# Layer 2's score products on the two halves of the array's rows, and C's product on quarters of the array

## Chip, cores, metric

One Trainium2 chip, one core of it in use. The metric is the device time of one execution in microseconds (us); lower is better.

## The reference

64 graphs of 256 nodes and width 512 pass four layers in f32. Every layer is `x = x + layer(relu(layernorm(x)))`. The change touches layer 2, which has 8 heads of width 64:

```python
Xp = einsum('bnd,hdk->bhnk', X, Wp) + bp
Xc = einsum('bhnk,hjk->bhnj', Xp, C)                                   # "C's product"
attn = tanh(A[:, None] * einsum('bhnj,bhmj->bhnm', Xc, Xp))            # "score products"
Xh = einsum('bhnm,bhmk->bhnk', attn, Xp)
out = relu(moveaxis(Xh, 1, 2).reshape(...))
```

Layer 0 and layer 3 gate a product by a softmax over nodes. Layer 1 is graph attention: its sums e_self[i] + e_neigh[j] are made by a small product with 40 rows.

## The kernel before

The weights stay on the chip, and each graph goes through all four layers there. Two graphs are interleaved; the build orders the instructions of both, so the order on an engine is not the written one. Two heads of 64 share the 128 partitions. To serve both with one product, the kernel pads with zeros: C is a 128x128 block with two 64x64 blocks on its diagonal, and Xc stands in a buffer whose other half of columns is zero for each head.

```python
    # The C of two heads on the diagonal of a block.
    c2_s = consts.tile([P, HP, P], F32)
    nc.gpsimd.memset(c2_s, 0.0)
    ...
    # Layer 2's Xc of two heads, apart by columns so that one product serves both.
    xc = consts.tile([P, HP, 2, N], F32)
    nc.gpsimd.memset(xc, 0.0)
    ...
        # layer 2, one graph; xpt is Xp transposed: [128 = two heads, pair of heads, node]
        for q in range(HP // 2):
            pc = passing("pc").rearrange("p (s n) -> p s n", s=2)
            for s in range(2):
                nc.tensor.matmul(pc[:, s, :], c2_s[:, 2 * q + s, :], xpt[:, 2 * q + s, :], start=True, stop=True)
            nc.vector.tensor_copy(xc[0:U, 2 * q:2 * q + 2, 0, :], pc[0:U])
            nc.scalar.copy(xc[U:P, 2 * q:2 * q + 2, 1, :], pc[U:P])
        ...
        for p in range(HP):
            th = []
            for m in range(NC):
                ps = passing("ps")
                nc.tensor.matmul(ps, xpt[:, p, m * P:(m + 1) * P], xc[:, p], start=True, stop=True)
                t = pairs.tile([P, 2, N], F32, name="th", bufs=6)
                nc.vector.tensor_tensor(t, ps.rearrange("p (s n) -> p s n", s=2),
                                        at[:, m, None, :].to_broadcast([P, 2, N]), OP.mult)
                nc.scalar.activation(t, t, AF.Tanh)
                th.append(t)
            if waiting is not None:
                spread(*waiting)      # the products with Xp for the pair of heads before
            waiting = (p, th)
```

Layer 1's product, whose two operands have 40 partitions (KE):

```python
                nc.tensor.matmul(ps, left[:, i * P:(i + 1) * P], right[:, 2 * p:2 * p + 2, :],
                                 start=True, stop=True)
```

## Time and profile before

| | before |
|---|---|
| time, median | 7153.95 us (7152.99 to 7154.43, 4 runs) |
| TensorE busy | 6468.8 us, 90% of the span |
| VectorE, ScalarE, GpSimd busy | 41%, 28%, 9% |
| mean granted clock of TensorE | 0.892 |
| score products, C's product | 510 us, 128 us busy |

How to read it. In the page's groups and in the timeline, a row names the line of the kernel, the engine, the operation, what it writes and reads, the shapes (partitions x elements), how many, and then busy time and mean ns of one (groups), or start and length in us (timeline, at the start of the row). L355 is the score product, L336 C's product, L287 layer 1's 40-row product. In the changed kernel they are L355, L334 and L282. A matmul's listed length is longer than what it costs in a stream (0.592 us listed for 512 columns, 0.429 to the next start), so costs are read from start to start. The lines themselves are in the prediction.

### The profile page before, as it was taken

The numbers are of one execution on the slowest core, as the hardware profiler recorded it, in microseconds if no ns is written. First come the engines' busy times: TensorE is split into PE (matmuls) and PEld (weight loads), VectorE is DVE, ScalarE is ACT, GpSimd is POOL, SyncE is SP. The second block draws the span as 40 slices with busy tenths as digits, with TensorE's granted clock in tenths as the row PEclk, the third lists the DMA queues.
The fourth block names the chain that finished last, engine by engine and source line by source line (L and its number), as shares of the span: only waits on it lengthen the run. The fifth ranks groups of instructions, "written<-read, shape, count | busy, mean of one in ns | idle before, by whom it ended". The sixth has DMA issues, their size and how long they took to land. (4 is left out here: it accounts for less than half of the span.)

```text
span 7152.9 us, 64137 instructions
## 1 busy us (share of the span) xinstructions
PE 6468.8 (90%) x24578; PEld 3687.2 (52%) x24578; DVE 2966.5 (41%) x7510; ACT 1997.0 (28%) x4801; POOL 671.6 (9%) x590
## 2 busy tenths in 40 slices
PE   7989999899998999989989999899989998999988
PEld 4555555555555555555555555555555554555554
DVE  4444444444444444434444344443444434444443
ACT  2222222222322222222222222232222222222222
POOL 1101001010010000100010001000010010100100
PEclk8988988889888898888988889888888888898889
DMA  2000000000000000000000000000000000000000
GB/s 66 15 11 12 12 11 15 12 11 12 11 15 12 11 15 8 15 12 11 15 11 12 15 8 15 11 12 15 8 15 12 11 15 11 12 12 11 11 6 6
DMA packets 55970, 95.80 MB, mean 13 GB/s; under 512 B 12080, under 2 KB 29040, under 8 KB 55664
## 3 DMA queue, kind: packets, MB, share of 16 engines
q1 hardware_dynamic: 34816, 50.34, 2.2%
q0 software_dynamic: 9216, 33.56, 1.2%
q10 hardware_dynamic: 11632, 7.80, 0.4%
q8 instruction: 195, 3.19, 0.2%
q14 instruction: 111, 0.91, 0.0%
HBM read 58.13 MB, written 33.55 MB: 13 GB/s over the span
## 5 line engine op out<-in xcount | busy, mean ns | idle before, releaser
L175 PE MATMUL pf<-wqk_s,ht 128*128 128x512 f32 x2048 | 1043.7, 659 | 0.0
L175 PE MATMUL pf<-w_s,ht 128*128 128x512 f32 x2048 | 981.4, 635 | 1.0
L175 PE MATMUL pv<-wv_s,ht 128*128 128x512 f32 x2048 | 945.2, 597 | 0.0
L167 PE MATMUL pt<-ident,hn 128*128 128x128 f32 x2048 | 414.3, 361 | 458.6 <-DVE hn L161 453.3
L281 PEld LDWEIGHTS po<-feats,et 128*128 128x128 f32 x4096 | 584.9, 218 | 314.4 <-ACT et L275 148.1
L299 ACT ACTIVATE e<-e,nmx 128x256 f32<-128x256 f32 x1024 | 510.3, 499 | 666.0 <-DVE nmx L296 665.9
L281 PE MATMUL po<-feats,et 128*128 128x64 f32 x4096 | 632.4, 305 | 43.9 <-ACT et L275 43.9
L175 PEld LDWEIGHTS pf<-wqk_s,ht 128*128 128x128 f32 x2048 | 418.2, 215 | 487.4 <-issue 487.2
L175 PEld LDWEIGHTS pf<-w_s,ht 128*128 128x128 f32 x2048 | 403.5, 203 | 514.4 <-issue 497.9
L287 PE MATMUL ps<-right,left 40*128 40x512 f32 x1024 | 660.1, 734 | 0.0
L167 PEld LDWEIGHTS pt<-ident,hn 128*128 128x128 f32 x2048 | 332.8, 192 | 544.4 <-issue 499.7
L168 ACT ACTIVATE ht<-pt 128x512 f32<-128x512 f32 x512 | 294.2, 596 | 1131.2 <-PE pt L167 1131.2
L291 ACT ACTIVATE e<-ps 128x512 f32<-128x512 f32 x512 | 305.7, 597 | 1073.6 <-PE ps L287 1069.4
L292 DVE TENSOR_TENSOR e<-ps,e 128x512 f32<-128x512 f32 x512 | 348.4, 685 | 549.4 <-ACT e L291 549.4
L348 PEld LDWEIGHTS ph<-xp,th 128*128 128x128 f32 x4096 | 492.5, 192 | 100.8 <-issue 69.1
L175 PEld LDWEIGHTS pv<-wv_s,ht 128*128 128x128 f32 x2048 | 364.6, 190 | 337.7 <-issue 337.7
L359 ACT ACTIVATE th<-th 128x512 f32<-128x512 f32 x512 | 321.2, 627 | 713.3 <-DVE th L357 713.3
L355 PE MATMUL ps<-xc,xpt 128*128 128x512 f32 x1024 | 510.1, 617 | 0.5 <-ACT xc L338 0.5
L277 DVE COPY et<-pt 128x512 f32<-128x512 f32 x256 | 177.0, 691 | 781.2 <-PE pt L271 781.2
L271 PE MATMUL pt<-ident,e 128*128 128x128 f32 x2048 | 387.8, 313 | 119.0 <-ACT e L299 117.3
L348 PE MATMUL ph<-xp,th 128*128 128x64 f32 x4096 | 495.3, 273 | 0.0
L271 PEld LDWEIGHTS pt<-ident,e 128*128 128x128 f32 x2048 | 255.0, 158 | 456.4 <-issue 186.8
(89 smaller groups left out, 5929.3 us busy)
## 6 DMA issues: line engine op xcount, KB each, us to landing
x_in<-in_x_dram SPq DMA_DIRECT2D x64, 512.0 KB, 3.4
out_dram<-xt POOLq DMA_DIRECT2D x64, 512.0 KB, 3.2
adj_in<-in_adj_dram SPq DMA_DIRECT2D x64, 256.0 KB, 2.7
wqk_s<-in_L_gnn_Wqk_dram ACTq DMA_DIRECT2D x1, 2048.0 KB, 10.6
wv_s<-in_L_gnn_W_v_dram ACTq DMA_DIRECT2D x1, 1024.0 KB, 9.7
w_s<-in_L_gnn_W_dram ACTq DMA_DIRECT2D x4, 256.0 KB, 8.5
w_s<-in_L_gnn_Wp_dram ACTq DMA_DIRECT2D x4, 256.0 KB, 6.5
wv_s<-in_L_gnn_Wv_dram ACTq DMA_DIRECT2D x1, 1024.0 KB, 12.5
```

The lines of the kernel that those rows point to most:

```text
L167: nc.tensor.transpose(pt[:, k * P:(k + 1) * P], hn[:, c, k * P:(k + 1) * P], ident)
L168: nc.scalar.activation(ht[:, :, c * P:(c + 1) * P], pt.rearrange("p (k i) -> p k i", k=KC), AF.Relu)
L175: nc.tensor.matmul(p, ht[:, k, c * P:(c + 1) * P], w[:, k], start=(k == 0), stop=(k == KC - 1))
L271: nc.tensor.transpose(pt[:, q * P:(q + 1) * P], e[:, s, j * P:(j + 1) * P], ident)
L281: nc.tensor.matmul(po[:, h * U:(h + 1) * U], et[:, s, j, :], feats[:, j, h * U:(h + 1) * U], start=(j == 0), stop=(j == NC - 1))
L287: nc.tensor.matmul(ps, left[:, i * P:(i + 1) * P], right[:, 2 * p:2 * p + 2, :], start=True, stop=True)
L291: nc.scalar.activation(e, psv, AF.Copy, scale=0.2)
L292: nc.vector.tensor_tensor(e, psv, e, OP.max)
L299: nc.scalar.activation(e[:, s, :], e[:, s, :], AF.Exp, bias=nmx[:, s:s + 1], scale=-1.0, accum_out=sums[:, 2 * p + s:2 * p + s + 1])
L348: nc.tensor.matmul(ph[n][:, h * U:(h + 1) * U], th[m][:, s, n * P:(n + 1) * P], xp[:, m, h * U:(h + 1) * U], start=(m == 0), stop=(m == NC ...
L355: nc.tensor.matmul(ps, xpt[:, p, m * P:(m + 1) * P], xc[:, p], start=True, stop=True)
L359: nc.scalar.activation(t, t, AF.Tanh)
```

## The change

Its intent: stop streaming zeros. Each head of a pair uses its own 64 rows of the array; the products of the two heads should run at once. For C's product each head uses a 64x64 quarter. Each half writes its own PSUM bank.

```diff
-    # The C of two heads on the diagonal of a block.
-    c2_s = consts.tile([P, HP, P], F32)
-    nc.gpsimd.memset(c2_s, 0.0)
+    c2_s = consts.tile([P, HP, U], F32)
     for s in range(2):
-        nc.scalar.dma_start(c2_s[s * U:(s + 1) * U, :, s * U:(s + 1) * U], ...)
+        nc.scalar.dma_start(c2_s[s * U:(s + 1) * U], ...)
@@ (xc and its zeros leave the constants; xc is now a working tile [P, HP, N])
         for q in range(HP // 2):
-            pc = passing("pc").rearrange("p (s n) -> p s n", s=2)
-            for s in range(2):
-                nc.tensor.matmul(pc[:, s, :], c2_s[:, 2 * q + s, :], xpt[:, 2 * q + s, :], start=True, stop=True)
-            nc.vector.tensor_copy(xc[0:U, 2 * q:2 * q + 2, 0, :], pc[0:U])
-            nc.scalar.copy(xc[U:P, 2 * q:2 * q + 2, 1, :], pc[U:P])
+            pc = [passing("pc").rearrange("p (a n) -> p a n", a=2) for _ in range(2)]
+            for a in range(2):
+                for s in range(2):
+                    half = slice(s * U, (s + 1) * U)
+                    nc.tensor.matmul(pc[s][half, a, :], c2_s[half, 2 * q + a, :],
+                                     xpt[half, 2 * q + a, :], start=True, stop=True)
+            nc.vector.tensor_copy(xc[0:U, 2 * q:2 * q + 2, :], pc[0][0:U])
+            nc.scalar.copy(xc[U:P, 2 * q:2 * q + 2, :], pc[1][U:P])
@@
         for p in range(HP):
+            ps = [passing("ps").rearrange("p (m n) -> p m n", m=NC) for _ in range(2)]
+            for m in range(NC):
+                for s in range(2):
+                    half = slice(s * U, (s + 1) * U)
+                    nc.tensor.matmul(ps[s][:, m, :], xpt[half, p, m * P:(m + 1) * P], xc[half, p, :],
+                                     start=True, stop=True)
             th = []
-            for m in range(NC):
-                ps = passing("ps")
-                nc.tensor.matmul(ps, xpt[:, p, m * P:(m + 1) * P], xc[:, p], start=True, stop=True)
-                t = pairs.tile([P, 2, N], F32, name="th", bufs=6)
-                nc.vector.tensor_tensor(t, ps.rearrange("p (s n) -> p s n", s=2), at[:, m, None, :]..., OP.mult)
+            for s in range(2):
+                t = pairs.tile([P, NC, N], F32, name="th", bufs=6)
+                nc.vector.tensor_tensor(t, ps[s], at, OP.mult)
                 nc.scalar.activation(t, t, AF.Tanh)
```

More of the change, by code (lines that the diff above doesn't have):

```diff
@@ L90, in tile_four_gnn_layers @@
     nc.scalar.dma_start(b2_bc, b2.rearrange("h u -> (h u)").partition_broadcast(P))
-    c2_s = consts.tile([P, HP, P], F32)
-    nc.gpsimd.memset(c2_s, 0.0)
+    c2_s = consts.tile([P, HP, U], F32)
     for s in range(2):
-        nc.scalar.dma_start(c2_s[s * U:(s + 1) * U, :, s * U:(s + 1) * U],
-                            c2t.rearrange("(a s) k j -> s k a j", s=2)[s])
+        nc.scalar.dma_start(c2_s[s * U:(s + 1) * U], c2t.rearrange("(a s) k j -> s k a j", s=2)[s])
     wqk3_s = load_weight("wqk3_s", wqk3)
@@ L135, in tile_four_gnn_layers @@
     nc.vector.tensor_copy(right[0:H], own[0:H, :, None].to_broadcast([H, H, N]))
-    xc = consts.tile([P, HP, 2, N], F32)
-    nc.gpsimd.memset(xc, 0.0)
     held = set()
@@ L331, in graph @@
             nc.scalar.copy(xpt[:, :, c * P:(c + 1) * P], pt.rearrange("p (k i) -> p k i", k=HP))
-        hold("layer 2")
+        xc = work.tile([P, HP, N], F32, name="xc")
         for q in range(HP // 2):
-            pc = passing("pc").rearrange("p (s n) -> p s n", s=2)
-            for s in range(2):
-                nc.tensor.matmul(pc[:, s, :], c2_s[:, 2 * q + s, :], xpt[:, 2 * q + s, :], start=True, stop=True)
-            nc.vector.tensor_copy(xc[0:U, 2 * q:2 * q + 2, 0, :], pc[0:U])
-            nc.scalar.copy(xc[U:P, 2 * q:2 * q + 2, 1, :], pc[U:P])
+            pc = [passing("pc").rearrange("p (a n) -> p a n", a=2) for _ in range(2)]
[6 more added lines that the diff above has]
+            nc.scalar.copy(xc[U:P, 2 * q:2 * q + 2, :], pc[1][U:P])
         yield
@@ L347, in spread @@
                     for m in range(NC):
-                        nc.tensor.matmul(ph[n][:, h * U:(h + 1) * U], th[m][:, s, n * P:(n + 1) * P],
+                        nc.tensor.matmul(ph[n][:, h * U:(h + 1) * U], th[s][:, m, n * P:(n + 1) * P],
                                          xp[:, m, h * U:(h + 1) * U], start=(m == 0), stop=(m == NC - 1))
         for p in range(HP):
-            th = []
-            for m in range(NC):
-                ps = passing("ps")
-                nc.tensor.matmul(ps, xpt[:, p, m * P:(m + 1) * P], xc[:, p], start=True, stop=True)
-                t = pairs.tile([P, 2, N], F32, name="th", bufs=6)
-                nc.vector.tensor_tensor(t, ps.rearrange("p (s n) -> p s n", s=2),
-                                        at[:, m, None, :].to_broadcast([P, 2, N]), OP.mult)
+            ps = [passing("ps").rearrange("p (m n) -> p m n", m=NC) for _ in range(2)]
[4 more added lines that the diff above has]
+                                     start=True, stop=True)
+            th = []
+            for s in range(2):
+                t = pairs.tile([P, NC, N], F32, name="th", bufs=6)
+                nc.vector.tensor_tensor(t, ps[s], at, OP.mult)
                 nc.scalar.activation(t, t, AF.Tanh)
@@ L365, in graph @@
         spread(*waiting)
-        held.remove("layer 2")
         xn = work.tile([P, NC, D], F32, name="xt", bufs=4)
```

## The prediction

> **What bounds the kernel now.** I read the page's busy table first, then the slices with the granted clock, the groups of instructions by line, the timeline of TensorE in the middle of the run, and the waits.
>
> ```profile
> span 7152.9 us, 64137 instructions
> ...
> PE 6468.8 (90%) x24578; PEld 3687.2 (52%) x24578; DVE 2966.5 (41%) x7510; ACT 1997.0 (28%) x4801; POOL 671.6 (9%) x590
> ...
> PEclk8988988889888898888988889888888888898889
> ...
> L287 PE MATMUL ps<-right,left 40*128 40x512 f32 x1024 | 660.1, 734 | 0.0
> ...
> L355 PE MATMUL ps<-xc,xpt 128*128 128x512 f32 x1024 | 510.1, 617 | 0.5 <-ACT xc L338 0.5
> ...
> L336 PE MATMUL pc<-xpt,c_s 128*128 128x256 f32 x512 | 127.6, 392 | 29.7 <-ACT xpt L331 28.7
> ```
>
> TensorE is busy 90% of the span and nothing else passes half of it apart from its own weight loads. The remaining 10%, 684 us, is idle time in front of a few lines. So time taken off TensorE is time off the span, except in places where TensorE would only wait longer for something else. The chain on the page covers only the last few per cent and carries nothing here. The two groups that the change touches are 510 us (score products) and 128 us (C's product), 9% of the span together. That is the ceiling of what can be discussed.
>
> Each f32 product appears as two weight loads and two matmuls: 64 graphs x 4 pairs of heads x 2 chunks are 512 score products, and the group counts 1024. The timeline gives the real rate, because the listed duration of one matmul includes a pipeline tail:
>
> ```profile
> 3548.43 1.95 PE L175 MATMUL pq<-wqk_s,ht 128*128 128x128 f32 x16
> 3550.21 1.88 PE L355 MATMUL ps<-xc,xpt 128*128 128x512 f32 x4
> 3551.93 2.74 PE L175 MATMUL pv<-wv_s,ht 128*128 128x512 f32 x6
> ```
>
> From the start of the four score matmuls to the start of the next group are 1.72 us, so 0.43 us for each 512-column matmul. (Subtracting the listed 0.592 of the last from 1.88 and dividing by three gives the same 0.429.) The 256-column matmuls of C's product follow each other at 0.216 us. Streaming of columns is what these cost; a weight load (0.19 us listed, one every 0.11 us where the 64-column products of layer 2 queue for it) hides behind it.
>
> The kernel already has a product on part of the rows, the 40-row sum of layer 1:
>
> ```profile
> 3508.70 1.12 PE L287 MATMUL ps<-right,left 40*128 40x512 f32 x2
> 3509.76 0.66 PE L271 MATMUL pt<-ident,e 128*128 128x128 f32 x4
> ...
> 3680.16 1.88 PE L355 MATMUL ps<-xc,xpt 128*128 128x512 f32 x4
> 3681.97 1.12 PE L287 MATMUL ps<-right,left 40*128 40x512 f32 x2
> 3683.02 1.98 PE L355 MATMUL ps<-xc,xpt 128*128 128x512 f32 x4
> 3684.84 1.89 PE L348 MATMUL ph<-xp,th 128*128 128x64 f32 x16
> ```
>
> Here the reader sees what a visit to another shape of the array costs. From 3680.16 to 3681.97 are 1.81 us where four matmuls stream in 1.72: 0.09 us are lost on entering the 40-row product. Its two matmuls last 1.05 us to the next start instead of 0.86; of the 0.19 too much, 0.10 is a weight load that could not run ahead (the second starts 1.12 - 0.59 = 0.53 after the first), and 0.09 is lost on leaving. The next full-array product again shows its first weight load: 1.98 instead of 1.88. So one visit loses 0.09 + 0.10 + 0.09 + 0.06 to 0.10, about 0.37 us.
>
> **What the Trainium skill says.** "TensorEngine Tiling (Array Packing)", section Key Properties: "Changing tiling mode (not just tile) drains the TensorE". The trace agrees, at the 0.37 us just read. "TensorE: Matmul & The Clock Gate", section "Part 3: Packing small matmuls — row/col tiling": matmuls on different row groups run concurrently, weight loads for another row group are pulled ahead, but matmuls start and end strictly in program order. No run so far shows two row groups at once; my main risk is here. "FP8 and Floating Point Precision", section "TensorE Precision Notes": true FP32 takes four passes. The trace agrees in effect: two instructions per product, each at 429 ns for 512 columns, twice the 213 ns that 512 columns take at the 2.4 GHz of the clock-gate page. "PSUM — Partial Sum Buffer", section "PSUM bank collisions raise a hardware error": row tiles must not write one bank at once. The change gives each half its own bank, so this is met, at the price that both banks are taken together.
>
> **The change part by part.** Score products. Before, per graph and pair of heads: 2 products with 512 columns, half of them multiplied by zeros, 4 matmuls x 0.429 = 1.716 us. After: 4 products of 64 rows with 256 columns, in the order (chunk 0, upper), (chunk 0, lower), (chunk 1, upper), (chunk 1, lower), each being two matmuls of 0.215. Perfect halving would give 4 x 0.215 = 0.86. But the two matmuls of one product sit on the same half and start in order, so only the second matmul of one product overlaps the first of the next: with four products this makes 4 + 1 = 5 units of 0.215, or 1.07 us. The eight weight loads at one per 0.107 to 0.112 us make 0.86 to 0.90 and just fit. Gain in streaming: 0.645 us per visit; each isolated visit pays 0.37 back, leaving 0.275.
>
> Now place by place, in a period of two graphs (about 223 us, 32 of them). In one half of the period the four visits start at 3550.21, 3558.83, 3562.50 and 3571.41; in the other at 3680.16, 3683.02, 3689.33 (split in two by transposes) and 3694.19.
> - Isolated visits 3550, 3558 and 3694: 3 x 0.275 = 0.83.
> - 3562.50: the next wait of TensorE is 1.77 us for hn, whose chain starts at the softmax transposes just before this visit. A shorter visit only makes that wait longer: 0.
> - 3571.41: stands before the 40-column product, whose change of shape is already paid, and TensorE is partly at half clock (2.55 us instead of 1.88): about 1.2 x 0.645 - 0.2 = 0.57.
> - 3680 and 3683 lie around a 40-row product that will have the same shape of tile, so no change between them: the visit that was paid for the 40-row product is paid once for all three, and both keep their 0.645: 1.3.
> - 3689.33: as a split visit 8 units become 6, 0.43, less two visits at 0.37: -0.31; if the order closes it up, +0.28. I take 0.
> Sum 2.7 us a period.
>
> C's product. Before 8 matmuls x 0.216 = 1.73 us per graph. It has no columns of zeros to save: it used one 128x128 block for two heads. After: 8 products, 16 matmuls on two diagonal quarters, so 8 + 1 units, 1.94 us, plus a change of shape on leaving; entering is free, since TensorE stands drained there today (0.86 us waiting for xpt). About 0.25 us more per graph, 0.5 a period.
>
> The rest: VectorE's multiplication and ScalarE's tanh keep 128 x 512 elements per instruction. The two evictions of C's product come from two banks and no longer wait for each other (ScalarE waits 142 us for VectorE there now), but TensorE hardly waits for them. The memsets of the zeros (1.8 us on GpSimd) lie beside the 22 us of first loads. All nothing.
>
> Total: (2.7 - 0.5) x 32 = 70 us, 1%: 7083 us.
>
> **The rivals.**
> 1. Weight loads bind. If a load for the other half is not pulled ahead of a matmul that itself still waits, each product costs 0.107 + 0.213 = 0.32 us instead of 0.215. A visit then streams 4 x 0.32 + 0.11 = 1.39, gaining 0.33 rather than 0.645: 8 visits give about 2.6 minus 2.5 of changes of shape, C's product loses some 0.6 a graph: 30 us slower, 7185. For it: in the full-array stretches a load starts only when the matmul before it starts. Against: the skill's description of loads drawn ahead for other row groups.
> 2. The halves do not run together in f32. Then 8 matmuls stream the old 1.72 us and every change of shape is a loss (2.2 us a period), and C's 16 matmuls take 3.44 instead of 1.73 (3.6 us a period): 186 us slower, 7340. For it: nothing seen in f32; against: the loads and matmuls name only rows they use.
> 3. Buffers. Both halves' banks are taken at once from a pool of four, so TensorE could wait for evictions by VectorE. For it: 24.3 us of load waits on th already stand in the list of waits, 32 times; against: VectorE is busy 41% and the same two banks per pair were in use before. Up to 0.5 us on one visit a period, 16 us.
> 4. The order. The instructions of the two graphs are interleaved by the build, not as written; if other products fall between the halves, each costs another 0.37 us and the overlap. One more such split per graph is 24 us plus the lost overlap of 14.
> 5. Better: if changes of shape cost less than in the 40-row product, the full 5.2 us of streaming a period would be 165 us, or 2.3%.
>
> **Range and chances.** Mechanism as computed 65% (7083, 50 either way), loads binding 20% (7185), no concurrency 7% (7340), better than computed 8% (7000). The middle of this mixture is about 7095. The range that should hold 8 in 10 is 7010 to 7200. Faster by over 2% means under 7010: 0.10; slower by over 2% means above 7296: 0.07; within 2%: 0.83.
>
> **What would show it.** In the timeline, a visit of eight score matmuls should last about 1.25 us to the next start where nothing waits, with a second half's first matmul starting within 10 ns of the first half's second; starts 0.32 apart would show rival 1, eight starts 0.215 apart rival 2. Busy time of the score group should fall from 510 to about 330 us, of C's product rise from 128 to about 145. Gaps of about 0.76 us in the loads before these visits show the changes of shape; fewer would be rival 5. The idle time before hn should rise by about 0.3 us on 32 occasions. A new wait of TensorE or its loads for th or xc would be rival 3. I am wrong if the time falls below 7010 or the score visits do not shorten at all.

## The result and the profile after

7042.88 us median (7041.81 to 7044.29, 4 runs) against 7153.95 before: 111 us less. The ratio is 0.9845, 95% interval 0.9831 to 0.9859. The time lies inside the predicted range, and "within 2%" came true. The point of 7095 was 52 us too high, the working's own 7083 was 40 us too high.

From the page of the changed kernel, the rows that answer to those shown of before:

```profile
span 7039.7 us, 67112 instructions
...
PE 6338.1 (90%) x26114; PEld 3644.4 (52%) x26114; DVE 2959.4 (42%) x7510; ACT 1995.7 (28%) x4801; POOL 669.3 (10%) x588
...
L282 PE MATMUL ps<-right,left 40*128 40x512 f32 x1024 | 656.9, 731 | 0.0
...
L347 PE MATMUL ph<-xp,th 128*128 128x64 f32 x4096 | 515.6, 277 | 28.3 <-ACT th L361 25.6
```

and from its groups, asked for by shape:

```profile
L355 PE MATMUL ps<-xc,xpt 64*128 64x256 f32 x2048 | 339.0, 439 | 0.0
...
L334 PE MATMUL pc<-xpt,c_s 64*64 64x256 f32 x1024 | 124.5, 382 | 29.6 <-ACT xpt L326 28.6
```

The score products went from 510 to 339 us of busy time, which the prediction had at about 330. C's product, which was to rise to 145, went from 127.6 to 124.5. The group ph, next in line behind the scores, got 28.3 us of idle time in front of it that it did not have: ScalarE's tanh is now sometimes not ready.

The timeline of TensorE (start, length; the same stretches of work as in the prediction):

```profile
3491.83 1.94 PE L334 MATMUL pc<-xpt,c_s 64*64 64x256 f32 x16
3493.70 2.05 PE L170 MATMUL pq<-wqk_s,ht 128*128 128x128 f32 x16
3495.68 1.13 PE L355 MATMUL ps<-xc,xpt 64*128 64x256 f32 x8
3496.75 2.84 PE L170 MATMUL pv<-wv_s,ht 128*128 128x512 f32 x6
...
3508.12 3.01 PE L347 MATMUL ph<-xp,th 128*128 128x64 f32 x24
3511.94 1.10 PE L347 MATMUL ph<-xp,th 128*128 128x64 f32 x8 [0.81 <-ACT th L361]
3514.33 1.94 PE L162 MATMUL pt<-ident,hn 128*128 128x128 f32 x8 [1.29 <-DVE hn L156]
...
3624.28 1.13 PE L355 MATMUL ps<-xc,xpt 64*128 64x256 f32 x8
3625.25 1.02 PE L282 MATMUL ps<-right,left 40*128 40x512 f32 x2
3626.11 1.21 PE L355 MATMUL ps<-xc,xpt 64*128 64x256 f32 x8
...
3631.12 0.70 PE L355 MATMUL ps<-xc,xpt 64*128 64x256 f32 x4
3631.97 1.10 PE L276 MATMUL po<-feats,et 128*128 128x64 f32 x8 [0.15 <-DVE et L272]
3633.01 0.70 PE L355 MATMUL ps<-xc,xpt 64*128 64x256 f32 x4
```

Four things are to be seen. A whole score visit takes 1.07 us to the next start (3495.68 to 3496.75) where it took 1.72. C's sixteen small matmuls take 1.87 us where its eight large ones took 1.83: each quarter's time is hidden under the other's. Between 3624.28 and 3626.11 no change of shape is paid: the 40-row product lasts 0.86 us, start to start, and not 1.05. And two visits, not one, are now split in two by other products (only one pair of halves at a time, at 3631.12 and 3633.01).

The single records of one visit, start times in us, read from the same trace:

```
3495.683 3495.689 | 3496.003 3496.009 | 3496.218 3496.225 | 3496.434 3496.441
```

Matmuls start in pairs 6 ns apart, and the pairs follow each other by 0.215 us (0.32 after the first, whose weight load shows). So the two halves run side by side from the first instruction to the last: 4 units of 0.215, not the 5 of the prediction.

**An account of one period.** The order of work repeats every two graphs. I took 23 such periods from the middle of each trace and split them three ways: *waits* are TensorE's idle time; the rest, from each matmul's start to the next, multiplied by the clock granted at that moment, is *work at full clock*; what is left is *lost to the half clock*. In us per period:

| | period | work | waits | lost |
|---|---|---|---|---|
| before | 221.87 | 183.52 | 20.04 | 18.31 |
| after | 218.45 | 180.50 | 20.64 | 17.31 |
| difference | -3.41 | -3.02 | +0.60 | -1.00 |

32 x (3.02 - 0.60) = 77 us of the gain are the change's own work and waits; 32 us come from the clock, which the prediction had left out. And one thing stands out: the edges at which the granted clock changes lie on a fixed grid of 3.413 us in every trace, and the period is 65.00 such windows before and 64.00 after. The gain per period is one window. This made the theory that the experiments had to test.

The lost time, shown by busy time per engine and granted clock (PEclk) in stretches cut at the clock's edges. First the kernel before, then the changed one, at the same place of the period:

```profile
core 0: us, PE busy (x) PEld busy (x) DVE busy (x) ACT busy (x) POOL busy (x), PEclk, DMA share, GB/s
3524.96:3528.37 3.41, 1.22 (x10) 0.97 (x8) 1.75 (x5) 1.23 (x4) 0.70 (x1) 1.00 0.00 0
3528.38:3538.61 10.23, 6.17 (x13) 3.42 (x14) 4.41 (x11) 1.19 (x2) 2.69 (x4) 0.50 0.13 51
```

```profile
3472.10:3475.51 3.41, 1.10 (x8) 0.97 (x8) 2.02 (x5) 0.97 (x4) 1.11 (x1) 1.00 0.00 0
3475.52:3482.33 6.81, 3.16 (x10) 2.40 (x11) 4.00 (x10) 1.19 (x2) 2.29 (x4) 0.50 0.20 77
```

Behind a window in which TensorE worked for a third of the time, the clock is halved, for three windows before and for two after.

### The profile page after: what moved, and what is told of

The parts are those of the page before. It is cut to its first block, busy times and chain, and to the rows that moved or that the text cites. A ratio compares the mean times of both kernels' runs of the same rounds, so it can differ in the third digit from the quotient of the medians.

```text
span 7039.7 us, 67112 instructions
## 1 busy us (share of the span) xinstructions
PE 6338.1 (90%) x26114; PEld 3644.4 (52%) x26114; DVE 2959.4 (42%) x7510; ACT 1995.7 (28%) x4801; POOL 669.3 (10%) x588
## 5 line engine op out<-in xcount | busy, mean ns | idle before, releaser
L170 PE MATMUL pf<-w_s,ht 128*128 128x512 f32 x2048 | 938.2, 612 | 1.0
L347 PE MATMUL ph<-xp,th 128*128 128x64 f32 x4096 | 515.6, 277 | 28.3 <-ACT th L361 25.6
L360 DVE TENSOR_TENSOR th<-ps,adj_t 128x512 f32<-128x512 f32 x512 | 334.6, 685 | 323.2 <-PE ps L355 323.2
```

The costliest lines, as they stand in the source:

```text
L170: nc.tensor.matmul(p, ht[:, k, c * P:(c + 1) * P], w[:, k], start=(k == 0), stop=(k == KC - 1))
L347: nc.tensor.matmul(ph[n][:, h * U:(h + 1) * U], th[s][:, m, n * P:(n + 1) * P], xp[:, m, h * U:(h + 1) * U], start=(m == 0), stop=(m == NC ...
L360: nc.vector.tensor_tensor(t, ps[s], at, OP.mult)
```

## The experiments

Three theories. *Own streams*: each half of the rows takes its matmuls by itself, against *program order*, the prediction's step. *Linear*: each us of TensorE work per period is 32 us of the time, against *whole windows* ("theory W"): the period settles at a number of throttle windows. Twelve kernels ran. The table has the accounts of all; the texts follow. "Windows" is the period divided by 3.4133 us.

| run | time | period | windows | work | waits | lost |
|---|---|---|---|---|---|---|
| scores_only | 7042.69 | 218.45 | 64.00 | 180.39 | 20.65 | 17.41 |
| c_only | 7150.72 | 221.87 | 65.00 | 183.62 | 20.06 | 18.19 |
| one_half | 7258.14 | 225.31 | 66.01 | 186.73 | 19.75 | 18.83 |
| upper_first | 7043.13 | 218.45 | 64.00 | 179.99 | 20.71 | 17.75 |
| after_full_p3 | 6990.86 | 216.82 | 63.52 | 179.22 | 20.71 | 16.89 |
| after_full_p23 | 6926.60 | 215.04 | 63.00 | 178.11 | 20.68 | 16.25 |
| after_full | 6715.93 | 208.21 | 61.00 | 177.32 | 20.81 | 10.08 |
| before_full | 6809.86 | 211.48 | 61.96 | 179.86 | 20.31 | 11.32 |
| before_warm | 6830.33 | 211.48 | 61.96 | 197.05 | 7.17 | 7.26 |
| after_warm | 7132.88 | 221.87 | 65.00 | 192.28 | 7.19 | 22.39 |
| best_warm | 6509.43 | 201.61 | 59.07 | 189.51 | 8.48 | 3.63 |
| before_best_warm | 6552.33 | 203.02 | 59.48 | 192.01 | 7.64 | 3.37 |

(The last four do 12.4 to 12.7 us of throw-away work per period, counted in their work.)

### The score part alone: scores_only

```diff
@@ against the changed kernel
-    c2_s = consts.tile([P, HP, U], F32)
+    c2_s = consts.tile([P, HP, P], F32); nc.gpsimd.memset(c2_s, 0.0)
     (the two blocks loaded onto the diagonal, as before)
-            pc = [passing("pc")... for _ in range(2)]
-            for a in range(2):
-                for s in range(2):
-                    nc.tensor.matmul(pc[s][half, a, :], c2_s[half, 2 * q + a, :], xpt[half, 2 * q + a, :], ...)
+            pc = passing("pc").rearrange("p (a n) -> p a n", a=2)
+            for a in range(2):
+                nc.tensor.matmul(pc[:, a, :], c2_s[:, 2 * q + a, :], xpt[:, 2 * q + a, :], start=True, stop=True)
```

> The score products on the two halves as in the changed kernel, C's product back on the zero-padded 128x128 block (8 matmuls instead of 16 per graph). The order of the instructions is the changed kernel's. In the traces C's product takes 3.76 us per two graphs before and 3.75 after, and the product behind it shows 0.1 us more after in one half of the period. So theory A (the quarters save and cost nothing, all of the gain is the score part): within 10 us of the changed kernel, 7043. My prediction's step (quarters cost 0.25 us a graph): 16 us faster, 7027.

7042.69 us (7041.88 to 7044.75), ratio to before 0.9844. All of the gain is the score part. The work per period is 0.11 us less than the changed kernel's, so the quarters cost about 0.05 us a graph, not 0.25.

### C's part alone: c_only

```diff
@@ against the kernel before
     (c2_s and the loop over q as in the changed kernel; the evictions into the padded xc)
+            nc.vector.tensor_copy(xc[0:U, 2 * q:2 * q + 2, 0, :], pc[0][0:U])
+            nc.scalar.copy(xc[U:P, 2 * q:2 * q + 2, 1, :], pc[1][U:P])
```

> C's product on quarters, the score products with zero padding as before; TensorE's order is the one of the kernel before. Theory A (quarters are free): within 5 us of before, 7154. My prediction's step (0.25 us a graph): 7170. If the two-graph period is held to whole windows of 3.413 us of the clock throttle (theory W), a small cost is swallowed and the time stays at 7154, or jumps by a whole window, 7260.

7150.72 us (7147.78 to 7153.77), ratio 0.9995, interval 0.998 to 1.001: the same. Work per period rose by 0.10 us and the loss to the clock fell by 0.12. The quarters are nearly free, and by themselves they bring nothing.

### Both heads on the same half: one_half

```diff
             for m in range(NC):
                 for s in range(2):
-                    half = slice(s * U, (s + 1) * U)
+                    half = slice(0, U)
```

> Wrong result on purpose: both heads' score products read the upper 64 rows, so all eight matmuls of a visit go to the same half of the rows; number, sizes, order and changes of shape stay. If the gain is the halves running at once: eight starts 0.215 us apart, a visit 0.86 us longer, 8 visits per two graphs, 32 periods: 220 us slower than the changed kernel, about 7263 (theory W: 64 windows become 66, 7261; no difference there). If the gain were only the smaller number of streamed columns per instruction or the weights, the time would stay at 7043.

7258.14 us (7250.3 to 7266.72), wrong result as intended, ratio 1.0144; 215 us slower than the changed kernel. One visit and what follows it in this run's timeline:

```profile
3602.40 1.99 PE L355 MATMUL ps<-xc,xpt 64*128 64x256 f32 x8
3604.32 2.84 PE L170 MATMUL pv<-wv_s,ht 128*128 128x512 f32 x6
```

The same eight matmuls, in the same order and shape, take 1.92 us instead of 1.07. So the gain is the two halves running at once in f32: without it work rises by 6.23 us a period, and the changes of shape leave this kernel slower than the one before. (Not all of the 215 us is that: 1.52 us a period more are lost to the half clock, and waits fall by 0.89.)

### The upper half first: upper_first

```diff
-            for m in range(NC):
-                for s in range(2):
+            for s in range(2):
+                for m in range(NC):
```

> The same four score products per pair of heads, both chunks of the upper half first, then both of the lower. If matmuls of the two halves start strictly in program order (my prediction's step), only the fourth matmul of the upper half overlaps the lower half's first: 7 units of 0.215 instead of 4 or 5 and a visit 0.65 us longer than the changed kernel's, 160 us slower, 7205. If each half has its own stream, which the pairs of starts 6 ns apart in the trace of the changed kernel suggest, nothing changes in a whole visit; the build also splits one or two visits fewer, so 7043 or up to 25 us less; held to whole windows, 7043 or 6934.

7043.13 us (7041.58 to 7043.64). A visit is as short as before:

```profile
3496.90 1.14 PE L355 MATMUL ps<-xc,xpt 64*128 64x256 f32 x8
3497.97 2.41 PE L170 MATMUL pv<-wv_s,ht 128*128 128x512 f32 x5
```

Its single starts come in pairs 14 ns apart (2841.545 and 2841.559, then 2841.865 and 2841.879, and so on). The lower half's first matmul, which stands behind four of the upper half in the program, starts 14 ns after the first of these. (That the build kept the program's order shows where it split a visit: two matmuls stand alone at 3633.05, the other six from 3634.04, and there, with two of the upper half left in front and not four, the lag is 6 ns.) So a half does not wait for the other's instructions: own streams, and the prediction's program order is refuted. The order with one split visit fewer also saved 0.51 us of work per period, 16 us by the linear theory. None of it arrived: the period stayed at 64.00 windows and the loss to the clock rose by 0.44. That speaks for whole windows.

### Layer 1's product on all rows: after_full_p3, after_full_p23, after_full, before_full

These take away changes of shape without touching the order or the sizes streamed: the 40-row product gets 88 more rows, all zero. The order on TensorE, VectorE and ScalarE is that of the kernel each is made from.

```diff
-    left = consts.tile([KE, N], F32)
+    left = consts.tile([P, N], F32)
-    right = consts.tile([KE, H, N], F32)
+    right = consts.tile([P, H, N], F32)
     (both are zeroed first, as they were)
@@ in after_full_p3 only for p == 3, in after_full_p23 for p > 1:
-                nc.tensor.matmul(ps, left[:, i * P:(i + 1) * P], right[:, 2 * p:2 * p + 2, :],
+                KR = P if p == 3 else KE
+                nc.tensor.matmul(ps, left[:KR, i * P:(i + 1) * P], right[:KR, 2 * p:2 * p + 2, :],
```

> The changed kernel with layer 1's 40-row product stretched to all 128 rows (the rows added are zeros) for the last of the four pairs of heads: no change of the array's shape there, order and everything else kept. Each such visit costs about 0.37 us more than a full-array product in the traces; 4 visits per two graphs, so 1.5 us less work of TensorE per period of two graphs. Linear theory (each us off TensorE's work per period is 32 us off the time): 6995. Theory W (the period is a whole number of throttle windows of 3.413 us; today 64): 7043, or 6934 with 63.

6990.86 us (6985.84 to 6991.14), ratio 0.9769.

> The same for the last two pairs: 8 visits per period, 3.0 us less work. Linear: 6948. Theory W: 7043 or, more likely, 6934.

6926.60 us (6926.0 to 6927.79), ratio 0.9681.

> The same for all four pairs: 16 visits, 5.9 us less work of TensorE; one visit that today shares its shape with the score products around it gains nothing and makes two new changes of shape, and one lies in a wait, so 4.8 us. Linear: 6890. Theory W: 6934 (63 windows) or 6825 (62).

6715.93 us (6714.68 to 6716.96), ratio 0.9387.

> The kernel before with the 40-row product on all 128 rows: no change of shape is left in it but the one of the 40-column product of layer 1. 15 visits outside waits at 0.37 us: 5.5 us less work per period. Linear: 7154 - 176 = 6978. Theory W: 7043 (64 windows) or 6934 (63). If changes of shape cost less than read from the trace, 7154 stays.

6809.86 us (6808.0 to 6810.38), ratio 0.9517.

The price of a change of shape holds up roughly. Work fell by 1.28 us for 4 visits a period, 2.39 for 8, so 0.30 to 0.32 us a visit (predicted 0.37); 3.18 for all 16, only 0.20 a visit, one of which lies between score products and gains nothing. In before_full, where no visit is shared, it is 3.66 for 16, or 0.23 a visit. The timeline of after_full shows the full-array product start to start in 0.86 us, with no loss behind it:

```profile
3502.28 1.02 PE L282 MATMUL ps<-right,left 128*128 128x512 f32 x2
3503.14 0.60 PE L266 MATMUL pt<-ident,e 128*128 128x128 f32 x4
```

My expectations of the time mostly missed. The first run broke theory W as I had stated it: the period is 63.52 windows, and its single periods alternate between 215.4 and 218.1 us in the middle of the trace (counted from C's product), so it is the pattern of two periods that settles, at 433.49 us or 127.00 windows. This run agrees with the linear figure as well (6995). The second fits 63.00. The third and fourth are far faster than either theory said: in after_full the work fell by 3.18 us a period but the loss to the clock by 7.23, and in before_full by 3.66 and 6.99. Waits hardly changed in either (20.8 and 20.3 us). The page of before_full shows the clock:

```profile
PEclk9999999999999999999999999999999999999999
```

So something other than idle time has a part in the throttle. The next runs point to what, though they were made for the older theory.

### Throw-away work in the waits: before_warm, after_warm, best_warm, before_best_warm

If waits cause the half clock, filling them should hold it up. Where TensorE waits 5.6, 5.0 and 3.4 us in each period, six, five and three useless products go into a bank that the transposes behind them overwrite. The build placed them in those waits, all but one.

```diff
-    def normed(xt):
+    def normed(xt, fill=0):
             pt = passing("pt")
+            for _ in range(fill if c == 0 else 0):
+                nc.tensor.matmul(pt, ident, wv0_s[:, 0], start=True, stop=True)
@@ before layer 2, and before layer 3 with 5
-        ht = normed(xt)
+        ht = normed(xt, 6 * (b % 2))
@@ in layer 1's gather
+                for _ in range(3 if b % 2 == 0 and i == 1 and a_pair == 0 else 0):
+                    nc.tensor.matmul(pt, ident, wv0_s[:, 0], start=True, stop=True)
```

> The kernel before, with throw-away products (six, five and three of 0.86 us, into a bank that the transposes behind them overwrite) where TensorE waits 5.6, 5.0 and 3.4 us in every period of two graphs, so that the granted clock need not fall. Theory W says that 18.3 us of a period of 221.9 are lost to the half clock that follows such waits, and that these losses adjust the period to whole windows. Without them: 183.5 us of work at full clock + 20.0 of waits = 203.6 a period, about 6570 in all. If the throttle does not matter, the throw-away products only cost time where they overrun their waits: 7154 to 7200.

6830.33 us (6828.88 to 6832.44), ratio 0.9548: a gain of 324 us, though not the 584 expected; 7.26 us a period are still lost.

> The changed kernel with the same throw-away products: 180.5 + 20.6 = 201.1 us a period, about 6490. What the change is worth by itself: with the clock held up the difference to the run before should be the work and the waits alone, 3.0 - 0.6 = 2.4 us a period, 77 us; if the 111 us measured were all the change's own, 111.

7132.88 us (7118.27 to 7146.94), ratio 0.997. The expectation failed badly: the changed kernel became 90 us slower by the same filling. Its stretches around one layer 2 show why (columns as above):

```profile
3653.54:3656.94 3.40, 3.40 (x20) 2.05 (x18) 1.98 (x3) 0.97 (x2) 0.00 (x0) 1.00 0.00 0
3656.96:3660.36 3.40, 3.31 (x20) 2.29 (x20) 2.58 (x7) 2.56 (x8) 0.00 (x0) 1.00 0.00 0
3660.37:3697.90 37.53, 35.21 (x127) 25.69 (x128) 16.21 (x37) 10.42 (x25) 2.19 (x2) 0.50 0.01 1
3701.33:3704.73 3.40, 3.40 (x9) 1.48 (x8) 0.00 (x0) 0.69 (x1) 0.00 (x0) 1.00 0.00 0
```

TensorE is busy 3.31 of 3.40 us in the second row, and still the clock is halved at its end, for 41 us in every period, while TensorE works on. What is low in that window is not busy time but how much of the array streams: half-row score products, the 40-row product, 64-column products that mostly wait for their weights, and changes of shape. I gave each matmul its streaming time (twice its columns at the granted clock) times the share of the 128 rows it names. In the window before the drop this comes to about 0.35 of the window; in the row above it, 0.70.

Over all fourteen traces, without their first windows, there are some 23,400 windows at full clock; 1,804 are followed by half clock. "This share below 0.37" tells the next window's clock in all but a few dozen of them (25 to 62, by how windows are cut). The same test by streaming time without the weight by rows fails in 219 at its best threshold, and by TensorE's busy time in 426. In 30 of the drops TensorE was busy over 90% of the window; all 30 are in after_warm, at this one place of the period. From the half clock it never came back behind a window whose share was under 0.61, and sometimes not behind 0.78. The threshold was fitted to these same records, not set up by an experiment of its own; after_full fits it, since its zero rows count as rows and it lost 7 us a period less.

> All that helped together: the changed kernel, upper halves first, layer 1's 40-row product on 128 rows and its 40-column product on 128 columns (zeros added), and the throw-away products. Work about 176.4 us a period, waits 20.8: 197.2, about 6370. If whole windows still rule, a multiple of 3.413 us near it, such as 58 windows = 197.97.

6509.43 us (6501.19 to 6513.84), correct, ratio 0.9098: the fastest version, 9% under the kernel before. Besides the parts named it differs by `wa` padded to 128 columns. The rows of its page:

```profile
PE 6191.1 (95%) x27010; PEld 3637.0 (56%) x27010; DVE 2952.7 (45%) x7510; ACT 1962.2 (30%) x4801; POOL 669.5 (10%) x588
...
PEclk9999999999999999999999999999999999999999
```

Work and waits are 198.0 as against 197.2 expected; the 3.6 us of loss are what was missed.

> The kernel before (score products padded with zeros, C's product on its block) with the 40-row product on 128 rows, the 40-column product on 128 columns and the throw-away products: the same surroundings as the fastest version, 6509 us, in which only 3.6 us of a period are lost to the half clock. So this pair shows what the change (with the upper halves first) is worth where the throttle does little. Work and waits as read: 3.0 us more work of TensorE than the fastest version and 0.5 us fewer waits, 2.5 us a period, 80 us: 6590; with whole windows (60 of 3.413 us are 204.8 us a period against 201.6), 6610. If the full-array products keep the clock up where the half-row products let it fall, this one could lose less to the half clock and come as low as 6480; then the change is worth nothing or less here.

6552.33 us (6552.05 to 6554.56), ratio 0.9161, against 0.9098. So in surroundings where the clock hardly falls the change, with the upper halves first, is worth 43 us: 32 x (2.50 of work - 0.84 of waits - 0.26 of loss) = 45. That is less than the 80 and 100 us of the first two expectations and more than the third, by which the change is worth nothing here; the waits that it brings back were put at 0.5 and are 0.84. Here the period is no multiple of the window (59.48 and 59.07): with 3.4 to 3.6 us lost a period there is little left by which the clock could stretch it.

## Why the prediction was right or wrong

**What bounds the kernel**: right. TensorE stayed at 90%, and no other engine passed half of the span.

**Streaming of a visit, "4 + 1 = 5 units"**: wrong, by the step that matmuls of the two halves start in program order. It is 4 units (pairs 6 ns apart; upper_first the same). This term was too long by one unit, 0.215 us a visit or 1.7 us a period. Rival 1 (weight loads bind) did not occur: the pairs follow each other at 0.215, not 0.32. Nor did rival 2 (no concurrency); one_half, where only the score part loses it, came to 7258, while the prediction's 2.2 us a period for that part give 7224.

**Changes of shape, 0.37 us a visit**: the size was about right for the score visits (about 0.4, below), somewhat high for the 40-row visits that were taken away (0.20 to 0.32). The shared visits around the 40-row product came as predicted.

**The split visit, taken as 0**: too favourable. The build split two visits in two, where the kernel before had one split (rival 4). upper_first, with fewer splits, has 0.51 us less work per period.

**C's product, 0.25 us a graph**: mis-sized. 0.05 measured, for the same reason as the first point.

**The hidden visit**: right. Where TensorE waited 1.77 us for hn, it now waits 0.81 for th and 1.29 for hn, 2.10 together: the 0.33 us are given back.

**Buffers (rival 3)**: no wait for a bank rose to matter; the new wait for th is for ScalarE's tanh.

**The sum**: 2.2 us a period predicted, 3.02 - 0.60 = 2.4 measured, 70 us against 77. That it came so near is luck: the errors of the steps cancelled. Taking the account's work apart by groups of matmuls, the score products' own work fell from 14.04 to 8.97 us, and that of the groups beside them rose by 2.3 (the ph products alone by 0.96), against which the other groups fell by 0.2. Halving eight visits of 1.716 us would give 6.86. So streaming gave 6.86 us, where the prediction's list has about 5.3; changes of shape, splits and C's product took back 3.8, not about 2.8 (0.1 of it C's, so about 0.4 for each of the ten visits or parts of visits); and waits took 0.6, not 0.3.

**What was missing altogether**: the granted clock as a term. It brought 1.0 us a period, 32 us, and made up most of the difference between 7083 and 7043. The prediction had only noted that TensorE is partly at half clock at one visit, and otherwise priced all at full clock. In this kernel the period settles at whole windows where much is lost to the clock: 65.00 to 64.00 with the change, 64.00 still with upper_first's 0.5 us less. Why it settles is argued, not shown: a period of another length would shift against the grid, and the loss would change until the lengths agree. And settling at half windows (after_full_p3) was not foreseen.

What stays open: whether the share of streaming rows is the throttle's own measure or only goes with it; and how long the change would keep its 77 us under another phase, since the same change gave 111 us, 94 us (before_full to after_full), 43 us (with the upper halves first), and a loss of 303 us (before_warm to after_warm) in four surroundings.

## What to carry to other kernels

Small products on separate halves of the rows do run side by side, each half on its own stream, but each visit to another shape of the array cost 0.2 to 0.4 us here; stretching a short product on few rows with zero rows, among neighbours on the full array, gained 327 us here, most of it from the clock. Account for TensorE's time as work at full clock, waits, and loss to the half clock before and after a change, because a few us of work can move the loss by as much or more, either way. When a gain equals a whole number of throttle windows per repeated pattern, it need not be the change's own size.

## What the Trainium skill lacked or had wrong

- "TensorE: Matmul & The Clock Gate", Part 3: matmuls are said to start and end strictly in program order. Across two row groups they did not: in upper_first the lower half's first matmul started 14 ns after the upper half's first, ahead of three that stand before it in the program.
- The same page, Part 1 and its part on HAM oscillation: the half clock is put down to idle gaps. Here it also followed windows in which TensorE was busy over 90% (3.31 of 3.40 us in after_warm), where the streaming time weighted by rows was under 0.37 of the window; and it never returned behind a window under 0.61. The 3.413 us window and the two clock values agree with the page.
- No page says that a repeating pattern can settle at whole windows: the period was 65.00, 64.00, 63.00 or 61.00 of them in eight of the fourteen kernels, and 18.3 of 221.9 us a period (8%) were lost to the half clock in the kernel before.
- "TensorEngine Tiling (Array Packing)", Key Properties: the drain at a change of tiling mode is right, but has no figure. Here 0.09 us on each side and 0.10 for a weight load that cannot run ahead; 0.20 to 0.32 us a visit when the 40-row visits were taken away, about 0.4 for the score visits.
- No page says that an f32 product appears as two matmuls, each with its own weight load, of 0.429 us for 512 columns at full clock. (Their sum, 0.858 us, agrees with the four passes of "FP8 and Floating Point Precision", section "TensorE Precision Notes", that the prediction cites.)
